# Gated cross-attention on one core: attention's products in two visits per quad instead of four, PSUM banks by pairs, inner sums first on GpSimd, softmax on ScalarE

## The chip, the cores and the metric

The kernel runs on one core of one Trainium2 chip. The metric is the device time of one execution in microseconds (us). Before the change three runs took 971.66, 971.86 and 970.93 us, median 971.66. One further execution was recorded by the hardware profiler; the views of its trace are the profile here. The engines are TensorE (PE; its weight loads are PEld), VectorE (DVE), ScalarE (ACT), GpSimd (POOL) and SyncE (SP, which issues DMAs). Each engine takes its instructions strictly in the order in which the program issues them.

## What is computed

All data is fp32. x is (8, 1024, 1024), the memory (8, 64, 512), W_mem (1024, 512), W_gate (1024, 2048).

```
memory_proj    = einsum('bme,de->bmd', memory, W_mem)
scores         = einsum('bnd,bmd->bnm', x, memory_proj) / sqrt(1024)
attn           = softmax(scores, axis=-1)
memory_context = einsum('bnm,bmd->bnd', attn, memory_proj)
gate_input     = concatenate([x, memory_context], axis=-1)
gate           = sigmoid(einsum('bnf,df->bnd', gate_input, W_gate) + b_gate)
fused          = x + gate * memory_context
out            = fused * rsqrt(mean(fused**2, axis=-1) + 1e-6) * norm_w
```

## The kernel before

**Set-up** (about the first 85 us) computes memory_proj and its product with the second half of W_gate, the bias added. Both halves of what attention multiplies then lie in one tile `mg` per batch: rows 0 to 63 hold memory_proj, rows 64 to 127 the gate's part. So attn times rows 0 to 63 gives the context (`pc`), and attn times rows 64 to 127 gives what must be added to the gate's sum.

**Quads.** The 8192 rows are taken in 16 quads of 512 rows, numbered `q`. A quad is 4 tiles of 128 rows: row half 0 (tiles 0, 1) and row half 1 (tiles 2, 3). Its x is loaded by `load_xq` and transposed by VectorE (`transpose_x`, line 355, eight instructions of 128x512 per quad) into the tiles `a11` to `a22`.

**Products.** x times the first half of W_gate is done with Winograd's form of Strassen's scheme on two levels. The outer level has 7 products in the order 1, 6, 7, 5, 4, 2, 3 (`ORDER`); their left sides are the `a` tiles and the sums S1 to S4 (`outer_s`, on VectorE). Each outer product (`outer_product`) has 7 inner products A, B, C, D, A', E, F, each a [128 x 256] result from two matmuls over 128 rows of contraction (each shows as two instructions, so four per inner product). The inner left sums `l` are made by GpSimd (`inner_s`, two parts of two instructions for the product that comes next). Inner results are combined by the chain p1 = A (copied by ScalarE, line 821), u2 = p1 + B, u3 = u2 + C, u4 = u2 + D on VectorE, and the blocks A + A', u3 + D, u3 + E, u4 + F are added into the output tiles `gate` (`O`). GpSimd first adds the SBUF parts (`pre`), VectorE then adds what lies in PSUM (`fin`, 256 columns each). An outer product feeds one or two quarters of the output (`sums`).

**Slots.** Every inner product is a slot: 7 per outer product, 49 per quad. `step()` runs at the start of a slot and issues whatever `at(slot, ...)` has put there, before that slot's matmuls; `mid((q, o), ...)` puts work into the middle of an outer product, after its visit. All instructions are pinned in the order of issue, so this order by hand is the order of every engine's queue. In quad q the products stand at slots 0 (1), 7 (6), 14 (7), 21 (5), 28 (4), 35 (2), 42 (3).

**Visits.** In the outer products 5, 4, 2 and 3, the last ones to add to a quarter of the output, attention's part is computed in a stretch between A' and E. Called a visit here, it has 8 matmuls over 64 rows for two tiles of 128 rows: 4 for `pc` from rows 0 to 63 and 4 for the gate from rows 64 to 127. In the trace they run as pairs, one on each half of the array. The gate's part goes straight into the banks of A, D, E and F. After product 3's visit the scores of the next quad follow (`scores`, 32 instructions `psT`, by `mid`).

**After a visit** the block is complete: ScalarE takes the sigmoid in place (`sigmoid`, line 668), VectorE multiplies by `pc` (`gated`), GpSimd issues a DMA that adds x (`residual`), ScalarE squares and takes the root (`square`, lines 682 and 687), and VectorE scales half a row at a time (`norm`, line 697), after which SP stores. The last quad has its own forms (`last_gated`, `last_root`, `last_norm`).

**Attention's weights.** `transpose_scores` (slot 9), `softmax_a` (10), `softmax_b` (13), `transpose_attn` (18) and `attn_difference` (21) turn the scores into `attnT`, the left sides of the visits. Maximum, subtraction, sum, reciprocal and scaling are on VectorE, the exponential on ScalarE.

**PSUM.** There are 8 banks: five banks b0 to b4 that go round for the inner products (one result of 256 columns each; the order changes with every outer product), two for `pc` (`ctx`, also a bank of set-up), and one for the scores and the transposes (`sc`). A tile can be written only when the last reader of what lay in its bank is done.

Of the kernel before, what the change touches and what calls it, by code (L numbers as in the profile page):

```python
# [15 lines left out]
P = 128  # L16
# [4 lines left out]
def tile_gated_cross_attention_rmsnorm(  # L21
# [89 lines left out]
    banks = [f"b{i}" for i in range(5)]  # L111

    def bank(n, shape, name):
        return ps.tile(shape, F32, tag=banks[n % 5], name=name)

# [3 lines left out]
    pz = bank(0, [P, C], "pz")  # L119
# [89 lines left out]
    pt = [bank(4, [P, BM], "pt0")]  # L209
    pt += [ps_ctx.tile([P, BM], F32, tag="ctx", name=f"pt{k}") for k in (1, 2)]  # L210
    pt += [ps.tile([P, BM], F32, tag="sc", name="pt3")]
# [20 lines left out]
    setup_banks = ["b0", "b1", "b2", "b3", "b4", "ctx", "ctx", "sc"]  # L232
# [109 lines left out]
    sTs, attns, attnTs, scs, mps, mgs = {}, {}, {}, {}, {}, {}  # L342
# [59 lines left out]
    def scores(q):  # L402

        pst = ps.tile([P, 2 * P], F32, tag="sc", name=f"psT{q}")
        mpb = mps[q // QPB]
        for k in range(KD):
            for r in range(2):
                mm(
                    pst[r * M : (r + 1) * M, :],
                    mpb[:, k, :],  # L410
                    A[q, r, k // KH][:, k % KH, :],
                    k == 0,
                    k == KD - 1,
                )
        sTs[q] = t4k(small, [P, 2, P], "sT", f"sT{q}")
        pin(nc.scalar.copy(sTs[q].rearrange("p t c -> p (t c)"), pst))

    def transpose_scores(q):
        sc = ps.tile([P, 4, M], F32, tag="sc", name=f"sc{q}")
        sT = sTs.pop(q)  # L420
        for t in range(2):
            pin(
                nc.tensor.transpose(  # L423
                    sc[:, 2 * t : 2 * t + 2, :].rearrange("p r m -> p (r m)"), sT[:, t, :], ident
                )
            )
        scs[q] = sc

    def softmax_a(q):
        sc = scs.pop(q)  # L430
        mx = t4k(small, [P, 4], "mx", f"mx{q}")
        pin(nc.vector.tensor_reduce(mx, sc, AX.X, ALU.max))
        e = attns[q] = t4k(small, [P, 4, M], "e", f"e{q}")
        tt(nc.vector, e, sc, mx.unsqueeze(2).to_broadcast([P, 4, M]), ALU.subtract)
        pin(nc.scalar.activation(e, e, AF.Exp, scale=SCALE))

    def softmax_b(q):
        e = attns[q]
        den = t4k(small, [P, 4], "den", f"den{q}")
        pin(nc.vector.tensor_reduce(den, e, AX.X, ALU.add))  # L440
        pin(nc.vector.reciprocal(den, den))
        tt(nc.vector, e, e, den.unsqueeze(2).to_broadcast([P, 4, M]), ALU.mult)

    def transpose_attn(q):
        attn = attns.pop(q)
        pa = ps.tile([P, 2, P], F32, tag="sc", name=f"pa{q}")
# [9 lines left out]
        at = attnTs[q] = t4k(small, [P, 6, P], "attnT", f"attnT{q}")  # L456
# [8 lines left out]
    def attn_difference(q):  # L465
        at = attnTs[q]
        tt(nc.vector, at[M:P, 4:6, :], at[M:P, 0:2, :], at[M:P, 2:4, :], ALU.subtract)

# [141 lines left out]
    ORDER = ((1, None), (6, None), (7, None), (5, (1, 1, 2)), (4, (1, 0, 2)), (2, (0, 0, 0)), (3, (0, 1, 4)))  # L610
    SLOTS = 49

    def plan(q):
        t0 = SLOTS * q
        nxt = q + 1 < NQ
        order = [o for o, _ in ORDER]
        for i, o in enumerate(order):
            for part, t in ((0, 1), (1, 2 if o == 7 else 5)):
                if i + 1 < len(order):
                    at(t0 + 7 * i + t, inner_s, q, order[i + 1], part)  # L620
                elif nxt:
                    at(t0 + 7 * i + t, inner_s, q + 1, order[0], part)
        if q == 0:
            at(t0 + 7, scores, q)
        at(t0 + (6 if q else 7), outer_s, q, 3)
        at(t0 + (20 if q else 7), outer_s, q, 4)
# [4 lines left out]
        at(t0 + 21, attn_difference, q)  # L631
# [4 lines left out]
        for t in (2, 3):  # L636
            mid((q, 5), transpose_x, q + 1, t, 0)
            mid((q, 2), transpose_x, q + 1, t, 1)
        for i, t, half in ((36, 0, 0), (38, 1, 0), (42, 0, 1), (43, 1, 1)):
# [124 lines left out]
    def outer_product(q, o, ext):  # L764

        nonlocal slot, banks
        l11, l12, l21, l22 = quarters(left(q, o))
        s1, s2, s3, s4 = (L2[q, o][:, i, :, :] for i in range(4))
        kb = {}

        def product(name, tag, lhsT, s, start=True):
            nonlocal slot
            step()
            if name not in kb:
                kb[name] = ps.tile([P, C], F32, tag=banks[tag], name=f"k{name}{q}_{o}")
            for k in range(2):
                mm(kb[name], lhsT[:, k, :], w_op(o, s)[:, k, :], start and k == 0, k == 1)
            slot += 1

        def o_blocks(row, h):  # L780

            for t in (2 * row, 2 * row + 1):
                if (q, t) not in O:
                    O[q, t] = t4k(gpool, [P, D], "gate", f"gate{q}_{t}")
            return [
                O[q, 2 * row + r][:, h * H + n * C : h * H + (n + 1) * C]
                for r in range(2)
                for n in range(2)
            ]


        sums = {
            1: [(o_blocks(0, 0), None)],
            6: [(o_blocks(0, 1), (0, 0))],
            7: [(o_blocks(1, 0), (0, 1))] if o == 7 else [],
            5: [(o_blocks(1, 1), (1, 0)), (o_blocks(0, 1), (0, 1))] if o == 5 else [],
            4: [(o_blocks(1, 0), (1, 0))] if o == 4 else [],
            2: [(o_blocks(0, 0), (0, 0))] if o == 2 else [],
            3: [(o_blocks(0, 1), (0, 1))] if o == 3 else [],
        }[o]  # L800
        sums = [(dst, src and o_blocks(*src)) for dst, src in sums]

        def pre(n, u):

            for dst, src in sums:
                if src is not None:
                    tt(nc.gpsimd, dst[n], src[n], u, ALU.add)

        def fin(n, name, u):
            for dst, src in sums:  # L810
                if src is not None:
                    tt(nc.vector, dst[n], (src if u is None else dst)[n], kb[name], ALU.add)
                elif u is not None:
                    tt(nc.vector, dst[n], u, kb[name], ALU.add)
                else:
                    pin(nc.scalar.copy(dst[n], kb[name]))
# [3 lines left out]
        product("A", 0, l11, R11)  # L820
        pin(nc.scalar.copy(p1, kb["A"]))  # L821
        product("B", 1, s2, T2)
        tt(nc.vector, u2, p1, kb["B"], ALU.add)
        product("C", 2, s3, R12)
        tt(nc.vector, u3, u2, kb["C"], ALU.add)
        pre(3, u3)
        pre(2, u3)
        product("D", 3, s1, T1)
        tt(nc.vector, u4, u2, kb["D"], ALU.add)
        pre(1, u4)  # L830
        product("A", 0, l12, R21, False)
        pcs = []
        if ext:
            row, h, g = ext
            at_, mg = attnTs[q], mgs[q // QPB]
            for n in ("E", "F"):
                kb[n] = ps.tile([P, C], F32, tag=banks[4 if n == "E" else 1], name=f"k{n}{q}_{o}")
            for r, names in ((0, ("A", "F")), (1, ("E", "D"))):
                pc = ps_ctx.tile([P, H], F32, tag="ctx", name=f"pc{q}_{o}_{r}")
                for n in range(2):  # L840
                    cols = slice(h * H + n * C, h * H + (n + 1) * C)
                    mm(
                        pc[:, n * C : (n + 1) * C],
                        at_[0:M, 2 * row + r, :],
                        mg[0:M, cols],
                        n == 0,
                        True,
                    )
                    mm(
                        kb[names[n]],  # L850
                        at_[M:P, g + r, :],
                        mg[M:P, cols],
                        names[n] in "EF",
                        True,
                    )
                pcs.append(pc)
        for fn in beside.pop((q, o), ()):
            fn()
        fin(0, "A", None)
        fin(3, "D", u3)  # L860
        product("E", 4, l22, T4, not ext)
        fin(2, "E", u3)
        if ext:
            sigmoid(q, 2 * row + 1, h)
            last = q + 1 == NQ
            if last:
                at(slot + 2, last_gated, 2 * row + 1, h, pcs[1])
            else:
                at(slot + 1, gated, q, 2 * row + 1, h, pcs[1])
        product("F", 1, s4, R22, not ext)  # L870
        fin(1, "F", u4)
        if ext:
            sigmoid(q, 2 * row, h)
            if last:
                at(slot + 3, last_gated, 2 * row, h, pcs[0])
            else:
                at(slot + 2, gated, q, 2 * row, h, pcs[0])
        if o in (4, 3) and q + 1 == NQ:
            c, d = 2 * ext[0], 2 * ext[0] + 1
# [7 lines left out]
        elif o in (4, 3):  # L887

            row = ext[0]
# [3 lines left out]
            if row == 0:  # L893
                when = (17, 18, 23, 29, None, None)
            else:
                when = (17, 18, 23, 25, 29, 32)
# [7 lines left out]
        banks = [banks[i] for i in (2, 3, 0, 4, 1)]  # L904
        del L2[q, o]

    for q in range(NQ):
        plan(q)
        for o, ext in ORDER:
            outer_product(q, o, ext)  # L910
# [29 lines left out]
```

## Time and profile before

| What | Value |
|---|---|
| median of three runs | 971.66 us |
| span of the profiled execution, first to last instruction | 969.8 us |
| time of the profiled execution around its span | not on the page |
| mean granted TensorE clock | 0.997 of full speed |
| from one quad's first scores matmul to the next's (298.68 to 353.53 in the chain) | 54.85 us |
| last TensorE matmul ends / last norm ends | 959.8 / 966.6 us |
| VectorE transpose, 128x512 (mean) | 1102 ns |
| VectorE sum of 256 / 512 columns with PSUM (mean) | 407 to 420 / 680 ns |
| VectorE half a norm (mean) | 926 ns |
| GpSimd sum of 256 columns into `gate` (mean) | 888 ns |
| ScalarE sigmoid of 512 columns (mean) | 631 ns |

A busy share is the time in which an engine had an instruction under way, divided by the span. The chain that ended last is followed back from the last instruction, at every step to what released it or to the instruction before it on its engine. A line of the timeline has the start in us, the duration in us, engine, line, operation, tiles (out<-in), shapes and how many were merged. A line of the waits says which engine and line waited for which, the total in us, how often, and the longest. An instruction's duration contains its start-up, so two back to back overlap: sums of 0.41 us follow each other every 0.33 us. Line 92 is the helper that issues all matmuls and line 95 the one that issues all tensor-tensor sums, so the tiles tell them apart.

### The profile page before, as it was taken

The numbers are of one execution on the slowest core, as the hardware profiler recorded it, in microseconds if no ns is written. First come the engines' busy times: TensorE is split into PE (matmuls) and PEld (weight loads), VectorE is DVE, ScalarE is ACT, GpSimd is POOL, SyncE is SP. The second block draws the span as 40 slices with busy tenths as digits, with TensorE's granted clock in tenths as the row PEclk, the third lists the DMA queues.
The fourth block names the chain that finished last, engine by engine and source line by source line (L and its number), as shares of the span: only waits on it lengthen the run. The fifth ranks groups of instructions, "written<-read, shape, count | busy, mean of one in ns | idle before, by whom it ended". The sixth has DMA issues, their size and how long they took to land.

```text
span 969.8 us, 14401 instructions
## 1 busy us (share of the span) xinstructions
PE 957.6 (99%) x4984; PEld 772.7 (80%) x4984; DVE 819.9 (85%) x1484; ACT 330.4 (34%) x604; POOL 763.5 (79%) x890
## 2 busy tenths in 40 slices
PE   9999999999999999999999999999999999999995
PEld 8546888788888888788888878788888878888884
DVE  6989879889797988879797978979797978979787
ACT  3000234161423334161433324152433325152345
POOL 4998868778786978878786978878687978878692
PEclk9999999999999999999999999999999999999998
DMA  9857483473919374482918375481917365391712
GB/s 374 273 144 172 88 139 91 118 165 77 173 66 172 111 130 99 111 173 69 182 66 162 101 136 114 102 182 57 193 66 150 112 133 118 88 195 50 189 66 87
DMA packets 70919, 128.32 MB, mean 132 GB/s; under 512 B 12352, under 2 KB 49216, under 8 KB 70592
## 3 DMA queue, kind: packets, MB, share of 16 engines
q1 hardware_dynamic: 61664, 93.86, 37.0%
q0 software_dynamic: 9184, 33.56, 18.8%
q8 instruction: 39, 0.64, 0.3%
q14 instruction: 32, 0.26, 0.1%
HBM read 87.56 MB, written 41.68 MB: 133 GB/s over the span
## 4 chain that ended last, share of the span: by engine, by line
PE 98%; DMA 1%; DVE 0%; ACT 0%; POOL 0%; SPq 0%; issue 0%; DVEq 0%
PE kA L92 20%; PE pc L92 12%; PE kE L92 11%; PE kD L92 10%; PE kF L92 10%; PE kB L92 10%; PE kC L92 10%; PE psT L92 6%; PE pg L92 5%; PE pm L92 2%; DMA wm<-in_w_mem_t 1%; PE pa L449 0%; PE sc L423 0%; DVE gate L755 0%; DVE gate L95 0%; ACT L762 0%
## 5 line engine op out<-in xcount | busy, mean ns | idle before, releaser
L95 POOL TENSOR_TENSOR gate<-gate,u 128x256 f32<-128x256 f32 x336 | 287.8, 888 | 106.9 <-DVE u L95 106.9
L668 ACT ACTIVATE gate<-gate 128x512 f32<-128x512 f32 x128 | 80.6, 631 | 306.3 <-DVE gate L95 305.7
L355 DVE STREAM_TRANSPOSE a<-xq 128x512 f32<-128x512 f32 x128 | 138.2, 1102 | 2.6 <-POOL it L95 2.6
L95 POOL TENSOR_TENSOR l<-a 128x256 f32<-128x256 f32 x128 | 121.7, 951 | 21.7 <-PE kA L92 21.7
L92 PE MATMUL pc<-mg,attnT 64*128 64x256 f32 x512 | 127.5, 389 | 0.0
L92 PE MATMUL kB<-it,l 128*128 128x256 f32 x448 | 115.1, 379 | 0.6 <-DVE gate L95 0.6
L92 PE MATMUL kD<-it,l 128*128 128x256 f32 x448 | 115.0, 379 | 0.0
L92 PEld LDWEIGHTS pc<-mg,attnT 64*128 64x128 f32 x512 | 90.6, 186 | 29.9 <-issue 21.2
L697 DVE SCALAR_TENSOR_TENSOR gate<-gate,ss,nw_sb 128x512 f32<-128x512 f32 x120 | 109.9, 926 | 1.1
L95 POOL TENSOR_TENSOR l<-s 128x256 f32<-128x256 f32 x96 | 79.2, 825 | 34.2 <-PE kF L92 34.1
L92 PE MATMUL kA<-w,a 128*128 128x256 f32 x384 | 98.6, 379 | 0.0
L92 PEld LDWEIGHTS kB<-it,l 128*128 128x128 f32 x448 | 85.0, 190 | 12.5 <-DVE gate L95 1.0
L92 PEld LDWEIGHTS kD<-it,l 128*128 128x128 f32 x448 | 85.1, 190 | 11.6
L95 DVE TENSOR_TENSOR gate<-gate,pc 128x512 f32<-128x512 f32 x128 | 87.0, 680 | 0.4 <-ACT gate L668 0.4
L95 DVE TENSOR_TENSOR gate<-gate,kE 128x256 f32<-128x256 f32 x112 | 45.6, 420 | 47.4 <-PE kE L92 41.4
L92 PEld LDWEIGHTS kA<-w,a 128*128 128x128 f32 x384 | 71.7, 190 | 9.5 <-issue 0.5
L821 ACT COPY u<-kA 128x256 f32<-128x256 f32 x112 | 40.6, 362 | 110.6 <-PE kA L92 106.3
L92 PE MATMUL kE<-it,a 128*128 128x256 f32 x256 | 69.0, 392 | 0.0
L682 ACT ACTIVATE junk<-gate 128x1024 f32<-128x1024 f32 x60 | 63.5, 1058 | 11.2 <-DMA gate<-in_x 10.2
L92 PE MATMUL kA<-t,s 128*128 128x256 f32 x256 | 65.8, 379 | 0.0
L92 PE MATMUL kF<-w,l 128*128 128x256 f32 x256 | 65.7, 379 | 0.0
L92 PE MATMUL kC<-w,l 128*128 128x256 f32 x256 | 65.7, 379 | 0.0
(143 smaller groups left out, 2042.6 us busy)
## 6 DMA issues: line engine op xcount, KB each, us to landing
xq<-in_x SPq DMA_DIRECT2D x64, 512.0 KB, 10.2
gate<-in_x POOLq DMA_DIRECT2D x60, 512.0 KB, 8.3
out<-gate SPq DMA_DIRECT2D x60, 512.0 KB, 2.6
w<-in_w_gate_t SPq DMA_DIRECT2D x8, 512.0 KB, 10.2
w<-in_w_gate_t SPq DMA_DIRECT2D x2, 2048.0 KB, 16.8
mg<-mgd SPq DMA_DIRECT2D x16, 256.0 KB, 3.8
wm<-in_w_mem_t SPq DMA_DIRECT2D x4, 512.0 KB, 6.4
mpd<-mpT SPq DMA_DIRECT2D x4, 512.0 KB, 7.1
```

Of the source, the lines that this page charges most:

```text
L92: pin(nc.tensor.matmul(o, lhsT, rhs, start=start, stop=stop, skip_group_check=True))
L95: pin(eng.tensor_tensor(o, a, b, op))
L355: nc.vector.transpose(A[key][:, :, r * P : (r + 1) * P], chunks(xq[q][:, 4 * t : 4 * t + 4, :], KD)[:, half * KH : (half + 1) * KH],)
L668: pin(nc.scalar.activation(g, g, AF.Sigmoid))
L682: nc.scalar.activation(junk, O[q, t], AF.Square, accum_out=ss[:, t % 2 : t % 2 + 1])
L697: nc.vector.scalar_tensor_tensor(g[:, cols], g[:, cols], rstd[:, t % 2 : t % 2 + 1], nw_sb[:, cols], ALU.mult, ALU.mult,)
L821: pin(nc.scalar.copy(p1, kb["A"]))
```

## The change

- A product has the order A, B, C, E, D, F, A'. The four results that form blocks lie in two banks: `af` holds A + A' and F, `ed` holds E and D. There are two such pairs, used in turn by the outer products. B lies in bank `b`, C in bank `c`.
- Products 5 and 2 are held: they get no visit of their own. In products 4 and 3, right after C, one visit does both: first the held product's attention (its `pc` in the banks b and c), then the current one's (its `pc` in `ctx`). Since D now lies on attention's part where u4 is read, a second difference of attnT (`NEG`, `attnT` 6 to 7) takes it out again. For product 3's visit the first `pc` is copied to SBUF (`pe`) by ScalarE, so that bank b can take the scores.
- The sums into the output are 512 wide: GpSimd's `pre` has one of 512 (u3, both blocks) and one of 256 (u4) per quarter, VectorE's `fin_ed` and `fin_af` one of 512 each in most cases.
- GpSimd's second part of the inner sums is issued at slot 2 of each product (it was slot 5 in all but one).
- Softmax: ScalarE takes the exponential for each of the four tiles with the maximum as bias and the sum as accumulator, and scales with the reciprocal. The score and transpose tiles use `ctx`, the scores themselves bank b.
- Transposes of the next quad's rows 2 and 3 move from the middle of products 5 and 2 to slots 24, 26, 40 and 41; that at slot 36 moves to 37. S3 moves from slot 6 to 3, S4 from 20 to 27 (in the first quad from 7 to 27). Gatings and norms move by a slot or so.

```diff
-    banks = [f"b{i}" for i in range(5)]
-
-    def bank(n, shape, name):
-        return ps.tile(shape, F32, tag=banks[n % 5], name=name)
-
+    def bank(tag, shape, name):
+        return ps.tile(shape, F32, tag=tag, name=name)
...
-        pst = ps.tile([P, 2 * P], F32, tag="sc", name=f"psT{q}")
+        pst = bank("b", [P, 2 * P], f"psT{q}")
...
+        pin(nc.vector.tensor_scalar(mx, mx, -SCALE, None, ALU.mult))
         e = attns[q] = t4k(small, [P, 4, M], "e", f"e{q}")
-        tt(nc.vector, e, sc, mx.unsqueeze(2).to_broadcast([P, 4, M]), ALU.subtract)
-        pin(nc.scalar.activation(e, e, AF.Exp, scale=SCALE))
+        den = dens[q] = t4k(small, [P, 4], "den", f"den{q}")
+        for t in range(4):
+            pin(
+                nc.scalar.activation(
+                    e[:, t], sc[:, t], AF.Exp, bias=mx[:, t : t + 1], scale=SCALE, accum_out=den[:, t : t + 1]
+                )
+            )
...
-        pin(nc.vector.tensor_reduce(den, e, AX.X, ALU.add))
         pin(nc.vector.reciprocal(den, den))
-        tt(nc.vector, e, e, den.unsqueeze(2).to_broadcast([P, 4, M]), ALU.mult)
+        for t in range(4):
+            pin(nc.scalar.activation(e[:, t], e[:, t], AF.Copy, scale=den[:, t : t + 1]))
...
+        tt(nc.vector, at[M:P, 6:8, :], at[M:P, 2:6:2, :], at[M:P, 3:6:2, :], ALU.subtract)
...
-            for part, t in ((0, 1), (1, 2 if o == 7 else 5)):
+            for part, t in ((0, 1), (1, 2)):
...
-        at(t0 + (6 if q else 7), outer_s, q, 3)
-        at(t0 + (20 if q else 7), outer_s, q, 4)
+        at(t0 + (3 if q else 7), outer_s, q, 3)
+        at(t0 + 27, outer_s, q, 4)
...
-        at(t0 + 21, attn_difference, q)
+        at(t0 + 22, attn_difference, q)
...
-        for t in (2, 3):
-            mid((q, 5), transpose_x, q + 1, t, 0)
-            mid((q, 2), transpose_x, q + 1, t, 1)
-        for i, t, half in ((36, 0, 0), (38, 1, 0), (42, 0, 1), (43, 1, 1)):
+        for i, t, half in (
+            (24, 2, 0), (26, 3, 0), (37, 0, 0), (38, 1, 0), (40, 2, 1), (41, 3, 1), (42, 0, 1), (43, 1, 1)
+        ):
             at(t0 + i, transpose_x, q + 1, t, half)
...
+    EXT = {5: (1, 1, 2), 4: (1, 0, 2), 2: (0, 0, 0), 3: (0, 1, 4)}
+    SECOND = {4: 5, 3: 2}
+    NEG = {4: 6, 3: 7}
...
+    def visit(q, o, pcs, af, ed):
+
+        row, h, g = EXT[o]
+        at_, mg = attnTs[q], mgs[q // QPB]
+        second = o in SECOND
+        for r, k in ((0, af), (1, ed)):
+            for n in range(2):
+                cols = slice(h * H + n * C, h * H + (n + 1) * C)
+                mm(
+                    pcs[r][:, n * C : (n + 1) * C],
+                    at_[0:M, 2 * row + r, :],
+                    mg[0:M, cols],
+                    n == 0,
+                    True,
+                )
+                left = NEG[o] if second and r == 0 and n == 1 else g + r
+                mm(k[:, n], at_[M:P, left, :], mg[M:P, cols], second and r == 1 and n == 0, True)
+
+    def pre(q, o, u3, u4):
+
+        for dst, src in SUMS[o]:
+            if src is None:
+                continue
+            if u3 is not None:
+                d, a = blocks(q, dst[0], 1, dst[1]), blocks(q, src[0], 1, src[1])
+                tt(nc.gpsimd, d, a, u3.unsqueeze(1).to_broadcast([P, 2, C]), ALU.add)
+            if u4 is not None:
+                d, a = blocks(q, dst[0], 0, dst[1]), blocks(q, src[0], 0, src[1])
+                tt(nc.gpsimd, d[:, 1], a[:, 1], u4, ALU.add)
...
+    def gate(q, t, h, pc, w):
+        sigmoid(q, t, h)
+        if q + 1 == NQ:
+            at(slot + w, last_gated, t, h, pc)
+        else:
+            at(slot + w, gated, q, t, h, pc)
...
+        step()
+        product(af[:, 0], l11, R11, True)
+        pin(nc.scalar.copy(p1, af[:, 0]))
+        step()
+        kb = bank("b", [P, C], f"kB{q}_{o}")
+        product(kb, s2, T2, True)
+        tt(nc.vector, u2, p1, kb, ALU.add)
+        step()
+        kc = bank("c", [P, C], f"kC{q}_{o}")
+        product(kc, s3, R12, True)
+        tt(nc.vector, u3, u2, kc, ALU.add)
+        pre(q, o, u3, None)
+        if second:
+            f = SECOND[o]
+            faf, fed, fu3, fu4 = held.pop((q, f))
+            frow, fh, _ = EXT[f]
+            fp = [bank(t, [P, H], f"pc{q}_{f}_{r}") for r, t in enumerate("bc")]
+            visit(q, f, fp, faf, fed)
+            if o == 3 and nxt:
+                pe = t4k(small, [P, H], "pe", f"pe{q}")
+                pin(nc.scalar.copy(pe, fp[0]))
+                fp[0] = pe
+            pcs = [ps_ctx.tile([P, H], F32, tag="ctx", name=f"pc{q}_{o}_{r}") for r in range(2)]
+            visit(q, o, pcs, af, ed)
+        if second:
+            one = slice(0, 1)
+            fin_af(q, f, faf, fu4, one)
+            gate(q, 2 * frow, fh, fp[0], 0)
+            fin_ed(q, f, fed, fu3, one)
+            gate(q, 2 * frow + 1, fh, fp[1], 1)
+            rest = slice(1, 2)
+            fin_af(q, f, faf, fu4, rest)
+            fin_ed(q, f, fed, fu3, rest)
         for fn in beside.pop((q, o), ()):
             fn()
...
+        step()
+        product(ed[:, 0], l22, T4, not second)
+        step()
+        product(ed[:, 1], s1, T1, False)
+        tt(nc.vector, u4, u2, ed[:, 1], ALU.add)
+        pre(q, o, None, u4)
+        first = o in SECOND.values()
+        if first:
+            held[q, o] = af, ed, u3, u4
+        else:
+            fin_ed(q, o, ed, u3)
+        if second:
+            row, h, _ = EXT[o]
+            gate(q, 2 * row + 1, h, pcs[1], 1)
+        step()
+        product(af[:, 1], s4, R22, False)
+        step()
+        product(af[:, 0], l12, R21, False)
+        if not first:
+            fin_af(q, o, af, u4)
+        if second:
+            gate(q, 2 * row, h, pcs[0], 1)
...
-                when = (17, 18, 23, 29, None, None)
+                when = (17, 18, 22, 28, None, 33)
             else:
-                when = (17, 18, 23, 25, 29, 32)
+                when = (17, 18, 22, 24, 29, 31)
```

## The prediction

> **What bounds the kernel now.** I read the page first: busy time, the clock row and the chain that ended last.
>
> ```profile
> span 969.8 us, 14401 instructions
> ...
> PE 957.6 (99%) x4984; PEld 772.7 (80%) x4984; DVE 819.9 (85%) x1484; ACT 330.4 (34%) x604; POOL 763.5 (79%) x890
> ...
> PEclk9999999999999999999999999999999999999998
> ...
> PE 98%; DMA 1%; DVE 0%; ACT 0%; POOL 0%; SPq 0%; issue 0%; DVEq 0%
> ```
>
> TensorE is busy for 99% of the span at full clock and is 98% of the chain, so only two things move the time: what TensorE itself takes, and new idle time on it. Its own part of the view of waits, and the chain of waits around the one wait in the loop, say what such an idle costs:
>
> ```profile
> PE kB L92 <- DVE gate L95: 0.6, 1, 0.6
> ```
>
> ```profile
> 111.00 1.10 DVE gate L95 x3
> 112.11 0.04 issue
> 112.15 0.92 PE kB L92 x3
> ```
>
> Here kB needs a bank that VectorE still reads; the matmul starts 0.05 us after VectorE's instruction ends, 0.8 us late. One such wait in the loop: all else is hidden.
>
> Next, TensorE's timeline over one visit (the short stretch of 64-row matmuls of the attention's products):
>
> ```profile
> 326.07 1.03 PE L92 MATMUL kA<-t,s 128*128 128x256 f32 x4
> 327.03 0.48 PE L92 MATMUL pc<-mg,attnT 64*128 64x256 f32 x1
> ...
> 327.35 0.38 PE L92 MATMUL pc<-mg,attnT 64*128 64x256 f32 x1
> ...
> 328.43 0.38 PE L92 MATMUL pc<-mg,attnT 64*128 64x256 f32 x1
> ...
> 328.64 0.38 PE L92 MATMUL pc<-mg,attnT 64*128 64x256 f32 x1
> ...
> 328.95 1.13 PE L92 MATMUL kE<-it,s 128*128 128x256 f32 x4
> 329.92 1.03 PE L92 MATMUL kF<-t,l 128*128 128x256 f32 x4
> ```
>
> Read the starts. Products follow each other at 0.865, pairs inside the visit at 0.21. Entering: 326.07 + 0.865 = 326.94, but pc starts at 327.03 (+0.09); the first pair takes 0.32 (+0.11). Leaving: 328.64 to 328.95 is 0.31 (+0.10); kE lasts 0.97 to kF's start (+0.10). A visit costs 0.40 beyond its work.
>
> Last, VectorE's timeline before the visit of product 3 in the same quad, because after the change that is what this visit will wait for:
>
> ```profile
> 342.41 1.12 DVE L355 STREAM_TRANSPOSE a<-xq 128x512 f32<-128x512 f32 x1
> 343.44 0.40 DVE L95 TENSOR_TENSOR u<-u,kD 128x256 f32<-128x256 f32 x1
> 343.73 2.12 DVE L355 STREAM_TRANSPOSE a<-xq 128x512 f32<-128x512 f32 x2
> ...
> 347.73 1.13 DVE L355 STREAM_TRANSPOSE a<-xq 128x512 f32<-128x512 f32 x1
> ...
> 349.34 1.12 DVE L355 STREAM_TRANSPOSE a<-xq 128x512 f32<-128x512 f32 x1
> 350.36 0.40 DVE L95 TENSOR_TENSOR u<-u,kB 128x256 f32<-128x256 f32 x1
> ```
>
> VectorE takes its queue in order, and the u2 sum (kB) stands behind transposes: it ends at 350.76, 1.0 us after its product was ready. That is free today: five banks go round, and nothing needs kB's bank soon.
>
> **What the change takes away.** Of 64 visits 32 go: 32 x 0.40 = 12.8 us. The wait of 0.8 in the first quad stood behind transposes and sums that move elsewhere: 0.8 more. Number and shape of the matmuls stay. Sum -13.6.
>
> **What it adds: the visit's banks.** The first matmul of a visit now writes bank b, which holds kB until u2 is read; its second half writes c, which holds kC until u3 is read. The visit starts right after product C, so u2 and u3 must be done within about one product. Queued behind TensorE's waiting matmul is all its work; so each lateness of u2 is paid in full. I follow VectorE's queue in its new order, from start to start of instructions back to back (timeline): 0.33 for 256 columns from PSUM, 0.60 for 512, 1.03 for a transpose, 0.80 (0.66 to 1.13) for half a norm. A sum starts 0.11 after its matmul's end, a product's end is 1.03 after its start.
>
> *From product 4's visit (start = 0) to product 3's.* TensorE: 16 pairs 3.55, then product E at 3.55, D 4.52, F 5.39, A' 6.25, product 2's A 7.11, B 7.98, C 8.84, E 9.71, D 10.57, F 11.44, A' 12.30, product 3's A, B, C 13.16 to 15.75; next visit due at 15.84.
> VectorE: product 5's four sums, 512 wide: the first may start at 1.24 (four pairs done), the second at 2.07, all issued by 3.87; half a norm 4.67; two gatings 5.87; u4 of product 4 6.20; its sum from bank ed 6.80; half a norm 7.60; gating of that half after its sigmoid (0.63 on ScalarE, ready 7.66) 8.26; sum from af 8.86; then VectorE idles for that half's sigmoid (8.97 to 9.60) because the gating is now due one slot earlier, ahead of u2: 9.72 to 10.32; u2 of product 2 10.65; transpose 11.68; u3 12.01; transpose 13.03; u4 13.36; four transposes in a row (slots 40 to 43; two of them stood behind product 2's visit before) 17.47; u2 of product 3 ends 17.88. TensorE goes at 17.93 instead of 15.84: **2.1 us idle**. Fifteen quads transpose for a next one: 31.5 us.
> Bounds: if VectorE were on time at u4 of product 2 (product D ends at 11.60, plus 0.11), u4, four transposes and u2 still end at 11.71 + 0.33 + 4.11 + 0.41 = 16.56: 0.8 idle is the floor. Upwards: norms at 1.13 (+0.6) and a late GpSimd sum (below, up to +0.7) give 3.4. I take 2.1, since every duration in it is a row.
>
> *From product 5's start (= 0) to product 4's visit, due at 8.73.* VectorE: product 7's sums end 0.94; reciprocal and half a norm 1.93; attention's differences, now two of 0.54, 3.0; u2, u3 3.66; transpose 4.69; u4 5.02; transpose 6.05; S4 (1.42 alone, 1.32 in a row), moved here from slot 20, 7.37; half a norm 8.17; u2 ends 8.58. Just in time: 0. But the copies of attnT, on which the differences wait, end 0.54 after product 5's start in half the quads and up to 2.5 after it in the others (ScalarE waits for the residual's DMA); that would give 0.4 to 0.9. The residual is issued after the transfer of xq has mostly landed now, so I take 0.15 on average, bounds 0 and 0.9: 2.3 us. The first quad has four inner sums there (0.79) and no norms (1.8 less): 3.2 - 1.8 - 0.1 = 1.3 once.
>
> **Edits costed at nothing, and their cover.**
> - GpSimd's 512-wide sums have no row in the loop: setup rows of that size take 1.27 to 2.27, two of 256 take 1.78. Seven per quad replace fourteen of 0.89: -3.6 to +3.4 on an engine at 79%. Cover: product 4's first sum is wanted at 6.20 and ready at 3.8 (cheap) to 7 (dear). Inner sums put first cost their own 1.5 per pair, inside that.
> - By the Trainium skill ("GPSIMD Engine Reference", 3.1 Elementwise, side-by-side cycle accounting) a two-input sum goes at about 2.6 cycles an element, an estimated 1.1 us for 512; with that the sum above would not change.
> - Softmax on ScalarE: four Exp of 64, each between 0.30 (a tiny Sqrt with bias) and 0.42 (Exp of 256) plus 0.19 to read the accumulator, four scaled copies of 0.30 to 0.37: 3.1 to 3.9 between slots 10 and 18, where TensorE has 6.9 us; uncovered, each us late would stop the transposes of slot 18. VectorE sheds 0.43 + 0.41 + 0.75 and adds 0.16.
> - The copy "pe" on ScalarE (0.59 by the 512-wide mg_c row) is ready about 1.9 after the visit's start, the scores want the bank at 3.55. The gating from it costs 0.79 instead of 0.68 in time that VectorE has under the scores.
> - Residual and output DMAs keep their slots within one; SP's queue passes none of them. Setup takes the same banks in the same order.
> - Tail: after the last matmul now 0.68 + 0.63 + 0.60 + 0.69 + 0.80 + 0.29 (the other half's root comes first), reciprocal and norms 3.2, and 0.3 of hand-overs: 7.2 to the last norm against 6.8 before (959.8 to 966.6): +0.4, bounds -1 and +1.
>
> VectorE's total falls (31 sums of 0.42 against 14 of 0.68 and 4 of 0.42 a quad), which helps nothing at the two places that TensorE waits at.
>
> **Does idling cost clock?** Row: after the idle of 0.8 the next matmuls go at 0.22 again and the clock row stays at 9. The skill ("TensorE: Matmul & The Clock Gate", "What's actually happening") has the clock halved after an idle window of about 3.4 us, which speaks against a change that brings idling; at 2.1 per visit its rule adds nothing. Were it to bite, a window at half clock would cost an estimated 1.7 a quad, 25 us in all.
>
> **Sum.** -13.6 + 31.5 + 2.3 + 1.3 + 0.4 = +21.9. The profiled execution has a span of 969.8 and the page gives no time around it; the median 971.66 is 1.9 above. I take that as what lies around: 969.8 + 1.9 + 21.9 = **993.6 us**.
>
> **Rivals.**
> 1. VectorE keeps up (the other side): u2 of product 3 is done before slot 44's product ends. Then only the gain is left: 971.7 - 13.6 + 0.4 = 958.5. For it: VectorE's lighter total. Against: the four transposes stand ahead of u2 in the queue. It decides at 13.6 / 15 = 0.9 us a quad.
> 2. Only the floor is paid, 0.8 a quad and nothing at product 4: 971.7 - 13.6 + 12 + 1.7 = 972; up to 1.4 a quad (without the wait for the sigmoid) 981. For it: norms at 0.66 when GpSimd is quiet.
> 3. Both places are late: 3.0 at product 3, 0.9 at product 4: -13.6 + 45 + 13.5 + 1.7 = +46.6, 1018. For it: late copies of attnT in half the quads.
> 4. Joining brings no saving, because changing banks inside a visit costs as much as entering it: +12.8, 1006. Against: in the rows the pair after the bank changes (328.43) keeps the 0.21.
>
> **How the numbers follow.** My case (1.5 to 2.9 idle a quad: 983 to 1008) 0.66; rival 1 0.12; rival 2 0.10; rivals 3 and 4 0.12. Range 970 to 1012: it leaves out rival 1 and most of rival 3. My case's own range is 983 to 1008. Faster by over 0.2% (about what three runs tell, 970.93 to 971.86): rival 1 and a little, 0.13; within 0.2%: the edge of rival 2, 0.03; slower 0.84.
>
> **What would show it.** After the change: 32 entries of 64-row matmuls, not 64; in the waits, PE pc waiting for DVE u, some 15 times 2 us, with L355 transposes just ahead of that u; TensorE's busy share near 95%; a quad's period (scores to scores) of about 56.3 instead of 54.85. Wrong if PE pc waits for nothing (rival 1), or if PE waits for ACT or POOL. The weakest step is the order of VectorE's queue before slot 44.

## The result and the profile after

The changed kernel takes 1016.25 us (median of 4 runs, 1015.73 to 1017.31) against 971.35 us (4 runs, 970.93 to 971.86): 1.0458 times as long, 95% interval 1.0444 to 1.0473. It is slower by 45 us, where 22 were forecast; the time lies 4 us above the stated range.

The page of the changed kernel, its busy times, clock row and chain:

```profile
span 1015.5 us, 14307 instructions
...
PE 948.5 (93%) x4984; PEld 779.5 (77%) x4984; DVE 816.0 (80%) x1260; ACT 366.5 (36%) x779; POOL 715.4 (70%) x778
...
PEclk9999999999999999999999999999999999999998
...
PE 54%; DVE 27%; ACT 9%; issue 9%; POOL 2%; DVEq 0%; ACTq 0%; POOLq 0%
```

TensorE has as many instructions as before, 9 us less busy time, and a share of 93%: it waits. The chain that was 98% TensorE now runs through VectorE for 27%, although VectorE itself is less busy than before. TensorE's own waits:

```profile
PE pc L92 <- DVE u L95: 52.7, 32, 2.0
PE af L92 <- ACT u L867: 1.2, 1, 1.2
```

So all 32 pairs of visits wait, and for the sums u on VectorE, as the prediction's main case has it. TensorE's timeline over one pair, in product 4:

```profile
399.83 1.03 PE L92 MATMUL kC<-t,l 128*128 128x256 f32 x4
402.65 0.48 PE L92 MATMUL pc<-mg,attnT 64*128 64x256 f32 x1 [1.79 <-DVE u L95]
...
402.98 0.38 PE L92 MATMUL pc<-mg,attnT 64*128 64x256 f32 x1
...
404.27 0.38 PE L92 MATMUL pc<-mg,attnT 64*128 64x256 f32 x1
...
404.49 0.38 PE L92 MATMUL pc<-mg,attnT 64*128 64x256 f32 x1
...
406.31 1.13 PE L92 MATMUL ed<-it,a 128*128 128x256 f32 x4
```

The first matmul of the visit starts 1.86 us later than kC's end allows (402.65 against 399.83 + 0.865 + 0.09). The second visit of the pair follows at 404.49, 0.22 after the last matmuls of the first: going from one visit to the next costs nothing. Taken from the starts in the whole trace, the wait of a normal quad is 1.86 us before product 4's pair and 1.71 before product 3's; together the 32 waits are 54.9 us.

What VectorE does ahead of each of the two. First up to product 4's pair of the same quad:

```profile
392.66 0.74 DVE L95 TENSOR_TENSOR gate<-gate,af 128x256 f32<-128x256 f32 x2
393.32 0.16 DVE L694 RECIPROCAL ss<-ss 128x2 f32<-128x2 f32 x1
393.51 1.23 DVE L698 SCALAR_TENSOR_TENSOR gate<-gate,ss,nw_sb 128x512 f32<-128x512 f32 x1
394.78 1.71 DVE L95 TENSOR_TENSOR attnT<-attnT 64x256 f32<-64x256 f32 x2
396.51 0.42 DVE L95 TENSOR_TENSOR u<-u,kB 128x256 f32<-128x256 f32 x1
...
399.74 1.39 DVE L95 TENSOR_TENSOR s<-a,s 128x1024 f32<-128x1024 f32 x1
401.06 1.21 DVE L698 SCALAR_TENSOR_TENSOR gate<-gate,ss,nw_sb 128x512 f32<-128x512 f32 x1
402.19 0.41 DVE L95 TENSOR_TENSOR u<-u,kB 128x256 f32<-128x256 f32 x1
```

From 392.66 on the queue has no gap of more than 0.15 us: the last u2 ends at 402.60 and TensorE starts at 402.65. Then up to product 3's pair:

```profile
412.31 0.69 DVE L95 TENSOR_TENSOR gate<-gate,pc 128x512 f32<-128x512 f32 x1 [0.69 <-ACT gate L669]
412.91 0.41 DVE L95 TENSOR_TENSOR u<-u,kB 128x256 f32<-128x256 f32 x1
...
415.88 4.07 DVE L352 STREAM_TRANSPOSE a<-xq 128x512 f32<-128x512 f32 x4
419.87 0.38 DVE L95 TENSOR_TENSOR u<-u,kB 128x256 f32<-128x256 f32 x1
```

VectorE idles 0.69 for the sigmoid, gates, and has six transposes and three sums before the u2 that TensorE needs.

**Where the 45.7 us of span come from** (1015.5 - 969.8). Visits that are gone: 32 x 0.40 = -12.8. Waits at the pairs: +54.9. A wait for p1 in the last quad: +1.4. Waits of before that are gone, in the first and the last quad: -0.8 and -0.7. One visit at half clock (below), 5.34 us long in place of 3.66: +1.7. From the last matmul to the end 11.9 instead of 10.0: +1.9. The sum is 45.6.

### The profile page after: what moved, and what is told of

It is laid out like the page before. It is cut to its first block, busy times and chain, and to the rows that moved or that the text cites. A ratio compares the mean times of both kernels' runs of the same rounds, so it can differ in the third digit from the quotient of the medians.

```text
span 1015.5 us, 14307 instructions
## 1 busy us (share of the span) xinstructions
PE 948.5 (93%) x4984; PEld 779.5 (77%) x4984; DVE 816.0 (80%) x1260; ACT 366.5 (36%) x779; POOL 715.4 (70%) x778
## 4 chain that ended last, share of the span: by engine, by line
PE 54%; DVE 27%; ACT 9%; issue 9%; POOL 2%; DVEq 0%; ACTq 0%; POOLq 0%
PE af L92 13%; PE pc L92 11%; DVE a L352 10%; PE ed L92 9%; PE psT L92 6%; PE pg L92 5%; DVE u L95 5%; DVE gate L698 4%; PE kC L92 3%; PE kB L92 3%; DVE gate L95 3%; PE pm L92 2%; ACT e L435 2%; ACT L435 2%; POOL gate L95 1%
## 5 line engine op out<-in xcount | busy, mean ns | idle before, releaser
L95 POOL TENSOR_TENSOR gate<-gate,u 128x512 f32<-128x512 f32 (+1 forms) x224 | 256.9, 1159 | 245.4 <-DVE u L95 211.5
L92 PE MATMUL ed<-it,l 128*128 128x256 f32 x448 | 115.0, 379 | 0.0
L92 PE MATMUL af<-w,a 128*128 128x256 f32 x384 | 98.5, 379 | 0.0
L95 DVE TENSOR_TENSOR gate<-gate,af 128x512 f32<-128x512 f32 (+1 forms) x128 | 77.4, 615 | 26.0 <-PE af L92 25.2
L92 PEld LDWEIGHTS ed<-it,l 128*128 128x128 f32 x448 | 83.9, 190 | 10.7
L95 DVE TENSOR_TENSOR gate<-gate,ed 128x512 f32<-128x512 f32 x112 | 76.4, 682 | 16.5 <-POOL gate L95 12.5
L92 PEld LDWEIGHTS af<-w,a 128*128 128x128 f32 x384 | 73.0, 190 | 10.3 <-issue 0.5
L92 PE MATMUL af<-mg,attnT 64*128 64x256 f32 x256 | 69.7, 393 | 0.0
L92 PE MATMUL ed<-it,a 128*128 128x256 f32 x256 | 67.4, 386 | 0.0
L92 PE MATMUL af<-w,l 128*128 128x256 f32 x256 | 65.8, 379 | 1.2 <-ACT u L867 1.2
```

The lines of the kernel that those rows point to most:

```text
L92: pin(nc.tensor.matmul(o, lhsT, rhs, start=start, stop=stop, skip_group_check=True))
L95: pin(eng.tensor_tensor(o, a, b, op))
```

## The experiments

The theory at the start: TensorE waits at a pair of visits for u2 in bank b, and u2 is late by what stands before it on VectorE. The rivals: that ScalarE or GpSimd make u2 late, that a pair of visits costs this whatever it writes, and that VectorE's total sets the period, so that a gain in one place is given back in another. In the table "quad" is the distance between the first scores matmuls of neighbouring quads, the waits are those of a normal quad before product 4's and product 3's pair.

| Kernel | Time, us | Against before (95%) | Quad, us | Product 4 | Product 3 |
|---|---|---|---|---|---|
| before | 971.7 | 1 | 54.85 | none | none |
| changed | 1016.25 | 1.0444 to 1.0473 | 57.6 | 1.86 | 1.71 |
| e_norms | 1022.2 | 1.0482 to 1.0544 | 57.3 to 59.7 | 1.9 | 1.45 |
| e_s4 | 1019.8 | 1.0458 to 1.0518 | 58.2 | 0.13 | 2.38 |
| e_inner | 1059.1 | 1.0796 to 1.0989 | 59.1 to 61.8 | 0 to 0.3 | 1.48 |
| e_softmax | 1013.7 | 1.0395 to 1.0455 | 57.5 | 1.70 | 1.71 |
| e_swap | 991.2 | 1.0164 to 1.0225 | 55.9 | 0 | 1.3 inside |
| e_late2 | 990.9 | 1.0162 to 1.0221 | 55.9 | 1.85 | 0 |
| e_late2_s4 | 971.8 | 0.9994 to 1.0016 | 54.6 | 0.12 | 0.43 |
| e_all | 965.2 | 0.9898 to 0.9956 | 54.2 | 0.12 | 0 |
| e_noinner | 994.7 | 1.0213 to 1.0251 | 56.3 | 0.55 | 1.71 |
| e_best | 964.6 | 0.9907 to 0.9934 | 54.2 | 0.12 | 0 |

### e_swap: is it the banks?

```diff
+            pcs = [ps_ctx.tile([P, H], F32, tag="ctx", name=f"pc{q}_{o}_{r}") for r in range(2)]
+            visit(q, o, pcs, af, ed)
             fp = [bank(t, [P, H], f"pc{q}_{f}_{r}") for r, t in enumerate("bc")]
             visit(q, f, fp, faf, fed)
...
-            pcs = [ps_ctx.tile([P, H], F32, tag="ctx", name=f"pc{q}_{o}_{r}") for r in range(2)]
-            visit(q, o, pcs, af, ed)
```

> The changed kernel with the two visits of a pair exchanged: the current product's first, with its context in the two banks kept for it, the held product's second, in banks b and c. Nothing else moves. Theory (the wait is for the banks b and c, until u2 and u3 are read): u2 and u3 have one visit (1.67 us) more, product 4's wait goes from 1.86 to about 0.2 us; VectorE's sums of the held product can't start earlier than now, so product 3's wait stays at about 1.7, inside the pair of visits; 990. Rival (starting a pair of visits costs that much whatever bank it writes): 1016 stays.

991.2 us. Product 4's pair starts with no wait at all; product 3's begins on time and waits 1.3 us in its middle, when it turns to bank b. The same matmuls in another order save 25 us, so starting a pair of visits has no such price of its own and the wait is for banks b and c. That rival is out.

### e_softmax: is it ScalarE's softmax?

```diff
-        pin(nc.vector.tensor_scalar(mx, mx, -SCALE, None, ALU.mult))
+        tt(nc.vector, e, sc, mx.unsqueeze(2).to_broadcast([P, 4, M]), ALU.subtract)
+        pin(nc.scalar.activation(e, e, AF.Exp, scale=SCALE))
...
+        pin(nc.vector.tensor_reduce(den, e, AX.X, ALU.add))
         pin(nc.vector.reciprocal(den, den))
+        tt(nc.vector, e, e, den.unsqueeze(2).to_broadcast([P, 4, M]), ALU.mult)
```

> The changed kernel with the softmax of before (subtraction, sum and scaling on VectorE). Theory (VectorE has caught up with TensorE at product 7's u3, so what happens in slots 10 to 14 is forgotten by product 4's visit): no change of either wait beyond 0.2 us; 1012 to 1020. Rival (softmax on ScalarE pushes the squares and the copies of attnT back, which delays the differences): product 4's wait falls by about 1 us, about 1000.

1013.7 us, and product 4's wait 1.70 in place of 1.86. The softmax on ScalarE costs some 2.5 us of the 45. That is little, as the theory has it.

### e_inner: GpSimd's inner sums in their old place

```diff
-            for part, t in ((0, 1), (1, 2)):
+            for part, t in ((0, 1), (1, 2 if o == 7 else 5)):
```

> The changed kernel with the second part of GpSimd's inner sums back at slot 5 of most products. Theory that VectorE's norm and differences before product 4's visit are slow (1.23 and 0.84 us against 0.75 and 0.51 alone) because GpSimd's inner sums run beside them: they speed up, product 4's wait falls to about 0.9; about 1003. Rival (the collisions only move to other sums, since GpSimd's work is the same): the waits stay within 0.3 us of 1.86 and 1.71; 1011 to 1021.

1059.1 us, the worst of all; neither expectation saw it. TensorE's waits in this kernel:

```profile
PE kC L92 <- POOL l L95: 53.6, 17, 3.3
PE pc L92 <- DVE u L95: 21.1, 15, 1.4
```

Product 4's C needs the inner sum s3, which now stands on GpSimd behind product 5's four sums into the output (in one place of the trace these take from 348.62 to 353.93, and s3's tile is done after that). Product 4's wait for u2 is nearly gone only because TensorE comes 3.3 us later. So this part of the change is needed by the rest of it. Half of what the theory supposed does show: the two differences of attnT take 0.42 each (in 31 of 32 cases), since the second pair of inner sums no longer stands beside them. The half norm before them stays at 1.23; the first pair, whose slot the change left as it was, still stands there. What this is worth can't be read from a kernel that waits elsewhere; e_noinner was made for that.

### e_noinner: do GpSimd's sums slow VectorE?

```diff
+        if o == 4:
+            L2[q, 4] = L2[q, 5]
+            return
         l11, l12, l21, l22 = quarters(left(q, o))
```

> The changed kernel without GpSimd's four inner sums for product 4, which takes product 5's instead (so this part of the computation is left out; all else runs as before). Theory (the norm and the two differences of attnT before product 4's visit take 1.2 and 0.84 us in place of 0.75 and 0.51 because GpSimd's inner sums run beside them): the differences fall to about 0.51 and the norm to about 0.75, u2 comes about 1.1 us earlier, product 4's wait falls from 1.86 to 0.7 to 0.9 us; about half of that comes back at product 3 as with S4 early; 1001 to 1009. Rival (they are slow for their second operand's address pattern or for another reason): the differences stay at 0.84; 1016 stays.

This kernel leaves out the four inner sums of product 4 and multiplies with product 5's instead. It takes 994.7 us. First GpSimd's timeline in the changed kernel, beside the stretch of VectorE shown above:

```profile
392.67 0.73 POOL L95 TENSOR_TENSOR l<-a 128x256 f32<-128x256 f32 x1
393.47 0.73 POOL L95 TENSOR_TENSOR l<-l,a 128x256 f32<-128x256 f32 x1
394.16 1.17 POOL L95 TENSOR_TENSOR l<-a 128x256 f32<-128x256 f32 x1
395.30 0.91 POOL L95 TENSOR_TENSOR l<-a,l 128x256 f32<-128x256 f32 x1
```

The four inner sums lie on the half norm (393.51) and the two differences (from 394.78). VectorE's timeline without them, in the stretch that answers to that one:

```profile
385.18 0.16 DVE L697 RECIPROCAL ss<-ss 128x2 f32<-128x2 f32 x1
385.37 0.75 DVE L701 SCALAR_TENSOR_TENSOR gate<-gate,ss,nw_sb 128x512 f32<-128x512 f32 x1
386.15 0.88 DVE L95 TENSOR_TENSOR attnT<-attnT 64x256 f32<-64x256 f32 x2
387.06 0.42 DVE L95 TENSOR_TENSOR u<-u,kB 128x256 f32<-128x256 f32 x1
...
391.61 1.21 DVE L701 SCALAR_TENSOR_TENSOR gate<-gate,ss,nw_sb 128x512 f32<-128x512 f32 x1
392.74 0.41 DVE L95 TENSOR_TENSOR u<-u,kB 128x256 f32<-128x256 f32 x1
```

The half norm takes 0.75 in place of 1.23, the two differences 0.88 in place of 1.71; the second half norm, which still has GpSimd's sums beside it, keeps 1.21. Product 4's wait falls from 1.86 to 0.55 us. The two savings, 0.48 and 0.83, are the whole fall of 1.31. Over all quads the 32 differences have a mean of 836 ns in the changed kernel and 422 here. Product 3's wait stays at 1.71, so nothing is given back, against the expectation's second half. Shown: two thirds of product 4's wait are instructions of VectorE that GpSimd's inner sums delay. The 0.83 comes from the second pair, which the change puts first (e_inner); the 0.48 comes from the first pair, whose slot it did not change.

### e_s4 and e_norms: VectorE's own work

```diff
-        at(t0 + 27, outer_s, q, 4)
+        at(t0 + (12 if q else 27), outer_s, q, 4)
```

> The changed kernel with S4 (1.4 us on VectorE) at slot 12 in place of 27, where VectorE idles 1.8 us for the exponentials. Theory (VectorE's own work): product 4's wait falls from 1.86 us to about 0.5, product 3's stays at 1.7; about 996. Rival (product 4's wait is set by the copies of attnT on ScalarE, which come late): VectorE waits for them instead, product 4's wait stays above 1.5; 1012 or more.

Product 4's wait falls to 0.13 us as expected (the copies of attnT do not take S4's place), yet the kernel takes 1019.8 us. Two things ate the gain. Half a norm after the first pair now meets GpSimd's 512-wide sum (1.65 us against 0.98 in the changed kernel), and product 3's wait grows by just that, from 1.71 to 2.38. And after a wait of this length TensorE goes at half speed; its timeline:

```profile
419.00 0.79 PE L92 MATMUL pc<-mg,attnT 64*128 64x256 f32 x1 [2.31 <-DVE u L95]
...
419.59 0.63 PE L92 MATMUL pc<-mg,attnT 64*128 64x256 f32 x1
...
421.72 0.63 PE L92 MATMUL pc<-mg,attnT 64*128 64x256 f32 x1
...
422.47 0.38 PE L92 MATMUL pc<-mg,attnT 64*128 64x256 f32 x1
```

Pairs are 0.42 apart in place of 0.21 until 422.15, which costs about 1.7 us. It happened in 12 of the 14 quads that wait 2.4 us there, some 20 us in all. The granted clock of the stretches 418 to 420, 420 to 422 and 422 to 424 was 0.73, 0.50 and 0.91; in the changed kernel it is 1.00 over the same numbers of its own span.

```diff
-                when = (17, 18, 22, 28, None, 33)
+                when = (17, 18, 22, 28, 45, 46)
```

> The changed kernel with the two half norms that stand between product 4's visit and product 3's moved to slots 45 and 46, under the scores. Theory (TensorE waits at each visit for u2 in bank b, and u2 is late by what VectorE has to do before it): product 3's wait falls from 1.71 us a quad to about 0.3, since 1.6 us of VectorE's work leave that stretch; product 4's stays at 1.86; 1016 becomes about 995. Rival (u2 is late because ScalarE or GpSimd is late, not by VectorE's own work): product 3's wait stays above 1.4, 1012 or more.

1022.2 us, a miss: product 3's wait falls by 0.26 only, to the 1.45 that the rival allowed. VectorE's timeline there shows why:

```profile
523.87 0.42 DVE L95 TENSOR_TENSOR u<-u,ed 128x256 f32<-128x256 f32 x1 [0.54 <-PE ed L92]
...
525.58 0.69 DVE L95 TENSOR_TENSOR gate<-gate,pc 128x512 f32<-128x512 f32 x1 [0.69 <-ACT gate L669]
...
527.56 0.69 DVE L95 TENSOR_TENSOR gate<-gate,pc 128x512 f32<-128x512 f32 x1 [0.70 <-ACT gate L669]
528.17 0.41 DVE L95 TENSOR_TENSOR u<-u,kB 128x256 f32<-128x256 f32 x1
```

With 1.6 us of work gone VectorE idles 1.9 us in place of 0.7, for product D and for two of ScalarE's sigmoids. So the rival is right in part: from the last sum of product 4 on it is a chain (sum, sigmoid, gating, u2, transposes) that runs through ScalarE too, and only what stands in that chain counts. Some quads got other waits of up to 0.9 us (five in all) and three visits went at half clock; what delays those quads was not followed further.

### e_late2, e_late2_s4, e_all, e_best: shortening the chain itself

e_late2 takes the last two transposes out of the chain; the scores need them only after the pair of visits, 3.7 us later.

```diff
-            (24, 2, 0), (26, 3, 0), (37, 0, 0), (38, 1, 0), (40, 2, 1), (41, 3, 1), (42, 0, 1), (43, 1, 1)
+            (24, 2, 0), (26, 3, 0), (37, 0, 0), (38, 1, 0), (40, 2, 1), (41, 3, 1)
...
         pre(q, o, u3, None)
+        if o == 3 and nxt:
+            transpose_x(q + 1, 0, 1)
+            transpose_x(q + 1, 1, 1)
```

> The changed kernel with the last two transposes (slots 42 and 43) issued after product 3's u3 in place of before its u2. Theory (product 3's wait is u2 behind VectorE's chain of sigmoid, gating, transposes): the chain gets 2.05 us shorter, product 3's wait of 1.71 goes to 0; product 4's stays at 1.86 or grows by up to 0.3; 988 to 993. Rival (what is gained at one visit is given back at the next, as with S4 early, since VectorE's work per quad sets the period): product 4's wait grows by more than 1 us; 1005 or more.

990.9 us: product 3's wait is 0, product 4's stays at 1.85. Nothing is given back, so VectorE's total does not bind.

e_late2_s4 is that and e_s4's edit.

> Both moves: the last two transposes after u3, and S4 at slot 12. Theory (two separate chains on VectorE, one before each visit; VectorE's total doesn't bind): waits of 0.1 at product 4 and 0.3 at product 3 (2.38 with S4 early alone, less 2.05), no throttled visits any more; a quad takes 54.5; 965 to 969, faster than before the change. Rival (VectorE's total binds): the waits come back in other places; above 980.

971.8 us, the time of before. The waits are 0.12 and 0.43, as expected to 0.13, and no visit is at half clock; a quad takes 54.6. The total is 3 to 7 us above the expectation, which had forgotten the waits of the first quad (2.0 us) and of the last one (0.4 and 1.5) and the longer end.

e_all adds:

```diff
-            gate(q, 2 * row, h, pcs[0], 1)
+            if nxt:
+                at(slot + 1, sigmoid, q, 2 * row, h)
+                at(slot + 2, gated, q, 2 * row, h, pcs[0])
+            else:
+                gate(q, 2 * row, h, pcs[0], 1)
```

> As the one before, and the sigmoid and the gating of the block that product 4 or 3 ends with come one slot later each, so that u2 of the next product stands ahead of them on VectorE and its p1 ahead of the sigmoid on ScalarE. Theory: the chain before product 3's visit gets another 0.9 us shorter, both waits are 0 to 0.2; a quad takes 54.2; 960 to 964. Rival: later gating holds the banks or the residual back, and a new wait stands at the transposes of slot 9 or at the squares; 966 or more.

965.2 us, between the theory's range and the rival's: product 3's wait is 0, a quad takes 54.2 as expected, and the kernel is 0.7% faster than before the change. 54.85 - 2 x 0.40 + 0.12 = 54.17: with the waits gone, the visits saved show in full.

e_best has S4 at slot 12 in the first quad too, and the later sigmoid also in the last quad's product 4:

```diff
+            if nxt or o == 4:
+                at(slot + 1, sigmoid, q, 2 * row, h)
+                if nxt:
+                    at(slot + 2, gated, q, 2 * row, h, pcs[0])
+                else:
+                    at(slot + 2, last_gated, 2 * row, h, pcs[0])
```

> The three moves together (last two transposes after product 3's u3, S4 at slot 12 in the first quad too, the last sigmoid and gating of products 4 and 3 a slot later), now with the later sigmoid in the last quad's product 4 too, so that the copy p1 of product 2 stands ahead of it on ScalarE. Theory: beside the 54.2 us a quad, the first quad's wait of 2.0 falls to about 0.7 and the last quad's wait of 1.7 for p1 goes; 961 to 964. Rival (the last quad is bound by its gatings and table loads whatever their order): 964 to 967.

964.6 us (5 runs, 964.09 to 964.88), 0.9921 of before (0.9907 to 0.9934). That is 0.6 above the theory's range and inside the rival's; from e_all's 965.2 (2 runs) it differs little. The first quad's wait falls from 2.0 to 1.1, not to 0.7. In the last quad the wait for p1 falls from 1.5 to 0.9, and the wait before its last pair grows from 0.4 to 1.1, so the last quad gains nothing, as the rival has it. TensorE's waits in it:

```profile
PE pc L92 <- DVE u L95: 2.5, 3, 1.1
...
PE af L92 <- ACT u L867: 0.8, 1, 0.8
```

## Why the prediction was wrong in size and right in kind

- **"A visit costs 0.40 beyond its work", 32 of them go: right.** 54.85 - 0.80 + 0.12 gives the quad of e_all. Rival 4 (joining saves nothing) is out: 404.27 to 404.49 is one normal step.
- **"The first matmul of a visit now writes bank b … each lateness of u2 is paid in full": right**, shown by e_swap.
- **Product 3's wait, 2.1 us with bounds 0.8 and 3.4: 1.71.** VectorE's walk had u2 end at 17.88 after product 4's visit began; it ended at 17.60 (402.65 to 420.25), the four transposes in a row being 0.12 quicker and the rest a little. TensorE's walk had the visit due at 15.84; it was due at 15.94, since the walk left out the 0.10 for leaving the first visit. e_late2 and e_all show that the transposes and the gating in this chain carried the wait. 15 x 0.4 = 6 us less than forecast.
- **Product 4's wait, 0.15 us "bounds 0 and 0.9": 1.86. This is the step that failed**, worth some 25 us (14 quads with 1.86 and the last with 1.16, against 15 x 0.15). The walk took the right instructions in the right order and priced them too low: u2 was to end 8.58 after product 5's start, and it ended at 10.54 (392.06 to 402.60). Product 7's sums "end 0.94" and ended at 1.26 (+0.32), since the first of them waited for a GpSimd sum of 512 columns, which took 1.66 us beside a half norm and takes about 1.28 with nothing of that kind beside it. The half norm took 1.27 from start to start in place of 0.80 (+0.47), "attention's differences, now two of 0.54" 1.73 in all in place of 1.07 (+0.66), the second half norm 1.13 in place of 0.80 (+0.33). These three read two tensors from SBUF, and a sum of GpSimd was under way when each began. Lastly u2 and u3 took 0.87 in place of 0.66 (+0.21), because u3 needs u2's result. I took the durations from places where GpSimd's sums were hardly in the way (the one difference of before takes 0.51 in nearly every quad). The upper bound came from late copies of attnT, which came close but did not bind: the norm ended at 394.74, the copies at 394.39.
- **"Inner sums put first cost their own 1.5 per pair, inside that": wrong.** They were costed as time on GpSimd alone. The cost of product 4's inner sums lay on VectorE beside them: 1.3 us at each product 4 (e_noinner).
- **The 512-wide GpSimd sums: within the bounds** of 1.27 to 2.27, mean 1398 ns. The 1.1 us estimated from the skill's page is too low: no such sum took less than 1.26. The negation of the maximum, costed at 0.16, took a mean of 861 ns for four columns; it is off the path.
- **"Does idling cost clock?": it did once** (+1.7 us, one of the 30 visits that waited 1.4 us or longer), where nothing was forecast. That it did not cost more is luck: the usual wait of 1.86 lies just under what the section on half clock below finds to be enough, and the 2.1 that I forecast lies above it. In e_s4, at 2.4, 12 of 14 such waits cost 1.7 each, the size that the prediction estimated.
- **First quad 1.3, tail +0.4:** the first quad's wait was 2.04, the tail grew by 1.9, and the last quad's waits of 1.2, 0.4 and 1.4 were not foreseen. In the tail VectorE reaches the last sum 1.8 us after the last matmul (1003.60 to 1005.44), because the gating of the other half stands before it; the walk had that half done earlier.
- **Rival 3 (1018) came out nearest in time, by luck**: it had waits of 3.0 at product 3 and 0.9 at product 4, where 1.7 and 1.9 were measured, and it put the second down to late copies of attnT.
- My case's own upper bound does not follow from its condition: 2.9 of idling a quad gives 1003 to 1006, not 1008.

## What to carry to other kernels

When a change lets the first instruction of a stretch on the bound engine wait for a short sum on another one, walk that engine's in-order queue back to the last point where it idles, and price each instruction by what is under way beside it in the new order, not by its mean. Take out of the queue what the waiting engine doesn't need yet (here two transposes, one gating, one sum), because only the chain ahead of the awaited instruction counts and not the engine's share. A change that loses by such waits may hold a gain: with three moves the same visits went from 1.046 to 0.992 of the time before.

## What the runs showed that I had not expected

**TensorE at half clock after short idling.** Over the twelve traces, of 117 single waits of 1.0 to 1.75 us in the loop none was followed by matmuls at double spacing, of 49 from 1.8 to 2.3 us four were, of 15 of 2.4 to 2.5 us thirteen, and of 16 of 3.4 us twelve. The slow stretch lasted 3.41 us, and three times in e_inner twice that. The Trainium skill ("TensorE: Matmul & The Clock Gate", "What's actually happening") puts the return to half clock after an idle window of about 3.4 us; the length of the slow stretch agrees, but here a shorter idle time is enough. It also says that the window runs freely. The traces fit that: where one has several slow stretches, all start a whole number of 3.413 us apart. Cut on this grid, 32 windows of the loop were followed by a slow one, and each held 1.9 us or more of TensorE's idling. Of the some 3070 other windows four held as much, 2.06 at most. So what counts here is, as far as these traces tell, the idle time inside one window, and a wait of 2.4 us that is split between two can go by without cost.

**VectorE beside GpSimd.** Instructions that read two tensors from SBUF are delayed by GpSimd's sums (differences 0.42 to 0.84, half a norm 0.75 to 1.65); the 512-wide sums with one input in PSUM take 0.68 and the transposes 1.09 beside GpSimd as well as without. The delay has a rule in these traces: the one that starts first is not delayed. A half norm that starts while a sum of GpSimd still has over 0.25 us to run ends 0.55 us after that sum's end (all 1031 cases, 0.54 to 0.55), and a difference 0.28 after (all 279). A half norm that starts with no sum under way takes 0.75, even when a sum starts during it (259 cases), and then it is the sum that takes longer. The lines at e_noinner show it: the sum from 393.47 ends at 394.20 and the half norm at 394.74. So the price is the rest of the GpSimd instruction under way, up to 1.1 us for a sum of 512 columns. The skill ("GPSIMD Engine Reference", 1. Specifications) has it that GpSimd shares its SBUF interfaces with VectorE and contends with instructions that have two inputs in SBUF. The runs agree. That sentence gives no price, but it names the instructions that the failed step had too cheap.
